# Products with B between the scans of a unit, and a quarter of unit five's product moved to VectorE

## The chip, the cores and the metric

The kernel runs on one core of one Trainium2 chip. The metric is the device time of one execution, in microseconds (us). The core has five engines that run side by side: PE (TensorE, matmuls), DVE (VectorE), ACT (ScalarE), POOL (GpSimd) and SP (SyncE, which here issues the DMAs). Each engine takes its instructions in order; where one engine needs what another makes, it waits on a semaphore.

## The reference

An image batch of shape (8, 64, 64, 96) passes through four layers, each of them added to its input after a group norm. Layers 0 and 2 are two-dimensional selective scans: the image is projected to 192 channels, convolved, and read as a sequence of 4096 positions in four directions; in each direction every channel carries 16 states:

```python
def step(h, inp):
    ut, dt, bt, ct = inp
    dA = jnp.exp(dt[..., None] * A4)
    dBu = (dt * ut)[..., None] * bt[:, :, None, :]
    h = h * dA + dBu
    y = jnp.einsum('bkdn,bkn->bkd', h, ct)
    return (h, y)
```

The four directions are added, normed, gated and projected back to 96 channels. Layer 1 is a scan of the same kind in a chunked form, layer 3 works on upsampled images (matmuls that stand for Fourier transforms). The change touches the scans of layers 0 and 2 alone.

## The kernel before

The images go through the kernel one after another; each has one call of `selective_scan` for layer 0 and one for layer 2, so there are 16 calls. A call has 32 steps: four directions k times eight chunks of 512 positions. A step has six units; a unit is 32 of the 192 channels with their 16 states. The 128 partitions of a unit's tiles are 4 states times 32 channels, and the other factor of 4 states lies along the columns as four groups of 512. A group has one place more, which carries the state in from the chunk before (`SEG` = 513).

A unit t, counted through all steps, with n = t % 6, takes these operations:

- `enter(t)` (ACT) writes the carried states into the free places of the tile `db`, which has three buffers.
- `spread(t)` (PE, L826) repeats the 32 rows of `du` (delta times u) over 128 partitions with a selection matrix, into the PSUM tile `pu`. `pu` has one buffer (pool `p_misc`, tag `misc`).
- `with_b(t)` (L832) multiplies that with B (tile `b`) into `db`, all four groups in one instruction of 128x2048. DVE does this for units 0, 1, 3 and 4, out of `pu`. POOL does it for units 2 and 5 (`n % 3 == 2`); POOL does not read PSUM here but takes `du2`, a copy of the rows 64 to 95 of `du` that goes to DRAM (`dud`) and comes back four times repeated by DMA.
- `decays(t, p)` (ACT, L847) writes the exponentials of two groups into `da[p]`. There is one `da` for each half p.
- `scan(t, p)` (DVE, L862) runs the recurrence over the two groups of half p, with `da[p]` and `db`, into `h`, which has five buffers.
- `leave(t)` keeps the last states (ACT, L878) and multiplies `h` with C (POOL, L883).

`total_y(i, hf)` (PE, L890 and L900) adds the states of units 3 hf to 3 hf + 2 of step i up: first one matmul that brings in what y holds, then 12 matmuls with the matrix `red`, each from 128 partitions to 32. Unit q of the three writes the band of rows 32 q to 32 q + 31 of the PSUM tile `py`. ACT copies `py` to `y` (L1001, L1011). The 12 are issued group by group, the three bands of a group next to each other.

`prepare(i)` is a generator that makes a step's inputs in eight parts: two matmuls into `pv` (L733, L743) and ACT's copies of them into `raw`, the DMAs that spread B, delta and C (`b`, `dx`, `c`, through DRAM), the softplus of delta (ACT, L767), and, in its seventh part, `du` on POOL (L785, where the chunk runs down columns of the image, otherwise L791) with the DMAs of `dud` and `du2`. `raw`, `du` and `du2` lie in the pool `soft`:

```python
tc.tile_pool(name="chunk", bufs=2) as cp,
tc.tile_pool(name="soft", bufs=1) as tp,
```

so that the next step's `du` is written over the one before. Parts of `prepare(i + 1)` and `prepare(i + 2)` are called in fixed places of the loop; the seventh is called by `leave` of unit 3 (`more`), ahead of unit 3's product with C.

`Beside` is a list of operations of layer 3 of the image before (matmuls on PE with an ACT operation behind each), three or four of which are put into each step. The first image has none, so that two of the 16 calls run without them.

The order on every engine is written out by hand (`tc.manual_schedule()`): it is the order of the calls in the loop over t at the end of `selective_scan`. In it, a unit's two scans stand next to each other on DVE, and a product with B follows behind the second.

Of the kernel before, what the change touches and what calls it, by code (L numbers as in the profile page):

```python
# [22 lines left out]
LC = 512  # L23
# [3 lines left out]
NSG = 4  # L27
# [40 lines left out]
def tile_vision_stack(  # L68
# [20 lines left out]
    nc = tc.nc  # L89
# [360 lines left out]
    def near(t, wh, at, n):  # L450

        if not wh:
            return t[:, at : at + n]
        return t.rearrange("p (h w) -> p h w", w=64)[:, :, at // 64 : (at + n) // 64]
# [5 lines left out]
    def cut(t, wh):  # L460

        return t.rearrange("p (w h) -> p w h", h=64) if wh else t
# [217 lines left out]
    def selective_scan(w, wdt, dgw, a, d, u, y, beside):  # L680
# [22 lines left out]
        total = len(steps) * units  # L703
        with (
# [11 lines left out]
            made = {}  # L716
            pool, ops = beside
            pool[0] = bp

            def prepare(i):  # L720

                k, c = steps[i]
                wh, at = k % 2 == 1, c * LC
                uv = [near(u[:, hf, :], wh, at, LC) for hf in range(2)]
                m = made[i] = {"dx": [], "du": []}
# [64 lines left out]
                else:  # L790
                    nc.gpsimd.tensor_mul(du, raw[:DM], u[:, :, at : at + LC])  # L791
                m["du"] = du
                dud = dp.tile([32, 2, LC], F32, name="dud")
                nc.sync.dma_start(dud, du[64:96])
                m["du2"] = du2 = tp.tile([128, 2, LC], F32, name="du2")
# [5 lines left out]
            def groups(t):  # L801

                return t[:, 1:].rearrange("p (g s) -> p g s", s=SEG)[:, :, :LC]
# [17 lines left out]
            def spread(t):  # L821

                m, n = made[t // units], t % units
                rows = slice(32 * (n % 3), 32 * (n % 3) + 32)
                m["pu"] = pu = pmp.tile([128, LC], F32, name="pu", tag="misc")
                nc.tensor.matmul(pu, sel[rows, :], m["du"][rows, n // 3, :], start=True, stop=True)  # L826

            def with_b(t):

                m, n = made[t // units], t % units  # L830
                pool = n % 3 == 2
                (nc.gpsimd if pool else nc.vector).tensor_mul(  # L832
                    groups(m["db", n]),
                    (m["du2"][:, n // 3, :] if pool else m["pu"])
                    .unsqueeze(1)
                    .to_broadcast([128, NSG, LC]),
                    m["b"],
                )

            def decays(t, p):  # L840

                i, n = t // units, t % units
                k, _ = steps[i]
                dst = das[p][:, 1:].rearrange("p (g s) -> p g s", s=SEG)
                for g in range(2):
                    gs = 2 * p + g
                    nc.scalar.activation(  # L847
                        dst[:, g, :LC],
                        made[i]["dx"][n // 3][:, n % 3, :],
                        AF.Exp,  # L850
                        scale=av4[:, k, n, gs : gs + 1],
                    )

            def scan(t, p):
                i, n = t // units, t % units
                k, _ = steps[i]
                rev = int(k >= 2)
                way = slice(None, None, -1) if rev else slice(None)
                at = slice(2 * p * SEG + rev, 2 * (p + 1) * SEG + rev)
                if p == 0:  # L860
                    made[i]["h", n] = gp.tile([128, NSG * SEG + 1], F32, name="h", bufs=5)
                nc.vector.tensor_tensor_scan(  # L862
                    made[i]["h", n][:, at][:, way],
                    das[p][:, rev : 2 * SEG + rev][:, way],
                    made[i]["db", n][:, at][:, way],
                    0.0,
                    ALU.mult,
                    ALU.add,
                )

            def leave(t, more):

                i, n = t // units, t % units
                k, _ = steps[i]
                h = groups(made[i]["h", n])
                if n == 0:
                    states[i] = stp.tile([128, NCG * NSG], F32, name="state")
                nc.scalar.copy(  # L878
                    states[i][:, NSG * n : NSG * n + NSG], h[:, :, 0 if k >= 2 else LC - 1]
                )  # L880
                if more:
                    prepare_part(i + 1)
                nc.gpsimd.tensor_mul(h, h, made[i]["c"])  # L883

            def total_y(i, hf):

                k, c = steps[i]
                wh = k % 2 == 1
                py = pyp.tile([128, LC], F32, name="py", tag="py")[:DM]
                nc.tensor.matmul(  # L890
                    py,
                    skip[:, hf, :] if k == 0 else ident[:DM, :DM],
                    near((u if k == 0 else y)[:, hf, :], wh, c * LC, LC),
                    start=True,
                    stop=False,
                )
                hs = [groups(made[i].pop(("h", 3 * hf + q))) for q in range(3)]
                for g in range(NSG):
                    for q in range(3):
                        nc.tensor.matmul(  # L900
                            turn_back(py[32 * q : 32 * q + 32, :], wh, LC),
                            red,
                            cut(hs[q][:, g, :], wh),
                            start=False,
                            stop=(g == NSG - 1),
                        )
                py = py.rearrange("p (h w) -> p h w", h=64) if wh else py
                return near(y[:, hf, :], wh, c * LC, LC), py

            going = {}  # L910

            def prepare_part(i):
                if i < len(steps):
                    if i not in going:
                        going[i] = prepare(i)
                    next(going[i], None)
# [26 lines left out]
                prepare_part(0)  # L943
            conv_half(5, 1, pmp, "misc")
            conv(w, y, u, (8, 24), 0)
            for _ in range(2):
                prepare_part(0)
            conv_half(6, 0, pyp, "py")
            for t in range(3):
# [16 lines left out]
            for _ in range(3):  # L966
                prepare_part(1)
            conv(w, y, u, (40, 48), 0)
            with_b(0)
            other = Beside(ops)  # L970
            for t in range(total + 2):
                n, i = t % units, t // units
                ahead = t + 1 < total
                quota = (i + 1) * len(ops) // len(steps) - i * len(ops) // len(steps)
                if n == 2 and quota > 1:
                    other.begin(pyp, "py")
                if n in (0, 3) and ahead:
                    spread(t + 1)
                elif n == 1 and t + 2 < total:
                    spread(t + 2)  # L980
                if n == 0 and i > 0:
                    sums = total_y(i - 1, 1)
                elif n == 3:
                    sums = total_y(i, 0)
                elif n == 4:
                    if quota > 3:
                        other.begin(pmp, "misc")
                    if t + 2 < total:
                        spread(t + 2)
                    prepare_part(i + 2)  # L990
                elif n == 5:
                    prepare_part(i + 2)
                if t < total:
                    scan(t, 0)
                    if n % 3 == 0 and t + 2 < total:
                        with_b(t + 2)
                if ahead:
                    decays(t + 1, 0)
                if n == 1:
                    if t > 1:  # L1000
                        nc.scalar.copy(*sums)  # L1001
                    if t < total:
                        other.begin(pyp, "py")
                elif n == 2:
                    other.end()
                    if quota > 2:
                        other.begin(pyp, "py")
                elif n == 3:
                    other.end()
                elif n == 4:  # L1010
                    nc.scalar.copy(*sums)  # L1011
                    other.end()
                if t < total:
                    scan(t, 1)
                    leave(t, n == 3)
                if t + 3 < total:
                    enter(t + 3)
                if ahead:
                    decays(t + 1, 1)
                    if (n + 1) % 3 != 2:  # L1020
                        with_b(t + 1)
                if n in (1, 2):
                    other.end()
                    if n == 2 and quota > 4:
                        other.begin(pyp, "py")
                if n in (4, 5):
                    prepare_part(i + 2)
                if n in (0, 1, 5):
                    prepare_part(i + 1)
            other.flush()  # L1030
            assert other.at == len(ops)
# [813 lines left out]
```

## Time and profile before

| | us |
|---|---|
| median of 3 runs | 26653.47 |
| lowest and highest of them | 26631.27, 26673.9 |
| the profiled execution's own time | 26693.06 |
| its span, first to last instruction | 26691.2 |
| DVE busy | 23982.3 (90%) |
| PE busy | 21984.9 (82%) |
| POOL busy | 21235.6 (80%) |
| ACT busy | 16407.9 (61%) |

The mean granted clock of PE over the span is 0.794 of full speed. In the profile a group's line has the source line, engine, operation, tiles and shapes, the number of instructions, the busy time in us and the mean time of one in ns, and then the time that the engine stood idle ahead of them, with what ended it. A timeline line has the start and the length in us; "x3" says that three instructions in a row were merged. A matmul in 32-bit floats shows as two records of each kind, one for each of two passes: PE for the passes themselves, PEld for the loads of their weights.

### The profile page before, as it was taken

What the parts mean: (1) busy time and instruction counts of PE and PEld (TensorE: products, weight loads), DVE (VectorE), ACT (ScalarE), POOL (GpSimd) and SP (SyncE); (2) the same over time, 40 slices, a digit from 0 to 9 for tenths busy, and PEclk for the clock granted to TensorE, in tenths of its full rate; (3) what the DMA queues carried; (4) which work ended last, traced back from release to release, by engine and by line L of the source; (5) the groups of instructions that cost most, each with busy time, mean ns of one, the idle gap of its engine ahead of it and who ended that gap; (6) DMA issues with size and microseconds to landing.
All of it is one profiled execution on the core that took longest, in us unless ns stands there. A gap on an engine that the chain in (4) does not pass through costs nothing. (4 is left out here: it accounts for less than half of the span.)

```text
span 26691.2 us, 282273 instructions
## 1 busy us (share of the span) xinstructions
PE 21984.9 (82%) x90981; PEld 8484.0 (32%) x90981; DVE 23982.3 (90%) x16689; ACT 16407.9 (61%) x29921; POOL 21235.6 (80%) x7928
## 2 busy tenths in 40 slices
PE   6796788888888878888888887888888888788888
PEld 2151222422224222242223422234222342223424
DVE  9989999898998989889898898988989889898896
ACT  5656566565665656556565565655656556565564
POOL 8949898497975979759797697976979769796694
PEclk7787777877778777787778877788777887778878
DMA  5515454154541545425453254532545325453352
GB/s 125 122 35 129 120 129 109 41 132 123 131 107 47 131 123 132 102 50 133 123 132 97 58 132 123 133 90 62 132 123 132 85 68 133 123 133 78 75 132 68
DMA packets 1678115, 2836.59 MB, mean 106 GB/s; under 512 B 434473, under 2 KB 477769, under 8 KB 1672033
## 3 DMA queue, kind: packets, MB, share of 16 engines
q1 hardware_dynamic: 1660000, 2812.23, 43.3%
q8 instruction: 731, 11.98, 0.2%
q10 hardware_dynamic: 16640, 6.29, 0.1%
q14 instruction: 744, 6.09, 0.1%
HBM read 2390.02 MB, written 427.49 MB: 106 GB/s over the span
## 5 line engine op out<-in xcount | busy, mean ns | idle before, releaser
L862 DVE TENSOR_TENSOR_SCAN h<-da,db 128x1026 f32<-128x1026 f32 x6144 | 13745.7, 2281 | 744.8 <-ACT da L847 378.5
L883 POOL TENSOR_TENSOR h<-h,c 128x2048 f32<-128x2048 f32 x3072 | 12743.1, 4172 | 968.2 <-ACT state L878 528.3
L900 PE MATMUL py<-h,cst 128*32 128x512 f32 x24576 | 5344.6, 749 | 473.0 <-POOL h L883 472.6
L847 ACT ACTIVATE da<-dx,a0s 128x512 f32<-128x512 f32 x6144 | 4239.6, 690 | 1548.8 <-DVE h L862 1373.0
L847 ACT ACTIVATE da<-dx,a2s 128x512 f32<-128x512 f32 x6144 | 4239.2, 690 | 1546.5 <-DVE h L862 1375.0
L832 POOL TENSOR_TENSOR db<-du,b 128x2048 f32<-128x2048 f32 x1024 | 4661.3, 4552 | 306.7 <-DMA du<-dud 226.5
L832 DVE TENSOR_TENSOR db<-pu,b 128x2048 f32<-128x2048 f32 x2048 | 4643.3, 2267 | 141.6 <-PE pu L826 138.2
L826 PE MATMUL pu<-du,cst 32*128 32x512 f32 x4096 | 2940.8, 805 | 1455.7 <-DVE db L832 927.4
L900 PEld LDWEIGHTS py<-h,cst 128*32 128x32 f32 x24576 | 1217.5, 133 | 4997.2 <-issue 3829.7
L826 PEld LDWEIGHTS pu<-du,cst 32*128 32x128 f32 x4096 | 735.2, 223 | 3145.9 <-DVE db L832 1580.8
L743 PE MATMUL pv<-u,wk 96*128 96x512 f32 x2048 | 1290.5, 762 | 388.1 <-ACT raw L738 388.1
L506 PE MATMUL ps<-s,w3as 96*128 96x512 f32 x1344 | 1069.4, 888 | 641.7 <-ACT sf L513 258.9
L1349 ACT ACTIVATE sg<-sg 128x768 f32<-128x768 f32 x1024 | 819.6, 800 | 862.2 <-PE sg L1333 862.2
L890 PE MATMUL py<-y,cst 96*96 96x512 f32 x1536 | 1306.1, 946 | 9.0 <-ACT y L1011 5.7
L733 PE MATMUL pv<-u,wk 96*96 96x512 f32 x2048 | 1200.9, 716 | 59.6 <-DVE u L281 27.4
L1303 POOL TENSOR_TENSOR ce<-ec,cr 112x512 f32<-112x512 f32 x256 | 521.5, 2037 | 754.9 <-ACT ec L1301 736.6
L1381 DVE TENSOR_TENSOR wt<-wt,cbm 128x768 f32<-128x768 f32 x1024 | 990.6, 1001 | 128.9 <-ACT wt L1350 128.1
L878 ACT COPY state<-h 128x4 f32<-128x4 f32 x3072 | 588.6, 192 | 796.5 <-DVE h L862 788.2
L526 PE MATMUL ps<-w3bs,sf 128*128 128x96 f32 x5376 | 1071.5, 356 | 0.0
L314 POOL TENSOR_SCALAR xn<-xs,sb 96x512 f32<-96x512 f32 x192 | 204.8, 1069 | 997.9 <-PE pz L319 440.8
L526 PEld LDWEIGHTS ps<-w3bs,sf 128*128 128x128 f32 x5376 | 992.9, 270 | 0.0
L738 ACT COPY raw<-pv 96x512 f32<-96x512 f32 x512 | 297.6, 581 | 970.1 <-PE pv L733 943.5
(238 smaller groups left out, 29900.9 us busy)
## 6 DMA issues: line engine op xcount, KB each, us to landing
dx<-dd SPq DMA_DIRECT2D x4096, 192.0 KB
b<-bcd SPq DMA_DIRECT2D x2048, 256.0 KB
c<-bcd SPq DMA_DIRECT2D x2048, 256.0 KB
du<-dud SPq DMA_DIRECT2D x2048, 128.0 KB
dd<-raw SPq DMA_DIRECT2D x1024, 192.0 KB
dud<-du SPq DMA_DIRECT2D x512, 128.0 KB
xd<-xs SPq DMA_DIRECT2D x256, 192.0 KB
cr<-bcd SPq DMA_DIRECT2D x1536, 32.0 KB
```

What stands on the lines that cost most here:

```text
L506: nc.tensor.matmul(ps, w3as[:, m * 128 : (m + 1) * 128], live["x2"], start=True, stop=True)
L526: nc.tensor.matmul(po, live["f"][m][:, at : at + 128], w2q[:, m, :], start=False, stop=(m == 2),)
L733: nc.tensor.matmul(pv[:DM], weights[k][:, hi, 128:], uv[hi], start=(hi == 0), stop=(hi == 1))
L743: nc.tensor.matmul(pv, weights[k][:, hi, :128], uv[hi], start=(hi == 0), stop=(hi == 1))
L826: nc.tensor.matmul(pu, sel[rows, :], m["du"][rows, n // 3, :], start=True, stop=True)
L832: (nc.gpsimd if pool else nc.vector).tensor_mul(groups(m["db", n]), (m["du2"][:, n // 3, :] if pool else m["pu"]) .unsqueeze(1) .to_broadc ...
L847: nc.scalar.activation(dst[:, g, :LC], made[i]["dx"][n // 3][:, n % 3, :], AF.Exp, scale=av4[:, k, n, gs : gs + 1],)
L862: nc.vector.tensor_tensor_scan(made[i]["h", n][:, at][:, way], das[p][:, rev : 2 * SEG + rev][:, way], made[i]["db", n][:, at][:, way], 0. ...
L883: nc.gpsimd.tensor_mul(h, h, made[i]["c"])
L890: nc.tensor.matmul(py, skip[:, hf, :] if k == 0 else ident[:DM, :DM], near((u if k == 0 else y)[:, hf, :], wh, c * LC, LC), start=True, st ...
L900: nc.tensor.matmul(turn_back(py[32 * q : 32 * q + 32, :], wh, LC), red, cut(hs[q][:, g, :], wh), start=False, stop=(g == NSG - 1),)
L1381: nc.vector.tensor_mul(it["wt"], it["wt"], m["cbm"][:, j : j + 1, :].to_broadcast([128, RK, Q]),)
```

## The change

Four things are changed.

1. The loop is written anew, so that a product with B stands on DVE between the two scans of each unit. Units 1 and 4 keep one instruction for all four groups; the products of units 0 and 3 are cut into two halves of two groups (`low`, `high`), which stand between the scans of the two units ahead of theirs.
2. Of unit five's product POOL makes three groups (`front`), and DVE makes the fourth (`last`), behind the second scan of unit 3. It reads `pu`, so that PE has one spread more in each step: after unit four's, in iteration n = 3.
3. `total_y` issues its 12 matmuls band by band, and is a generator that stops after two of the three bands; the third is issued later. Unit five's spread stands between them, and unit zero's follows behind the third band.
4. `prepare` has nine parts: `du` is a part of its own, called by `leave` of unit 2 in place of unit 3 and ahead of unit 2's product with C; `dud` and `du2` come at the end of iteration 5. Other parts and the operations of `Beside` have new places in the loop, and `Beside` no longer uses the `misc` tile.

The core of the diff:

```diff
                 m["du"] = du
+                yield
                 dud = dp.tile([32, 2, LC], F32, name="dud")
...
+            low, high, last, front = slice(0, 2), slice(2, 4), slice(3, 4), slice(0, 3)
+
+            def with_b(t, part=slice(None)):
                 m, n = made[t // units], t % units
-                pool = n % 3 == 2
+                pool = n % 3 == 2 and part != last
+                out, b = groups(m["db", n])[:, part], m["b"][:, part]
...
-                hs = [groups(made[i].pop(("h", 3 * hf + q))) for q in range(3)]
-                for g in range(NSG):
-                    for q in range(3):
+                for q in range(3):
+                    h = groups(made[i].pop(("h", 3 * hf + q)))
+                    for g in range(NSG):
                         nc.tensor.matmul(
...
+                    if q == 1:
+                        yield
                 py = py.rearrange("p (h w) -> p h w", h=64) if wh else py
-                return near(y[:, hf, :], wh, c * LC, LC), py
+                yield near(y[:, hf, :], wh, c * LC, LC), py
...
+                if n == 0:
+                    with_b(t + 2)
+                    if i > 0:
+                        adding = total_y(i - 1, 1)
+                        next(adding)
+                elif n == 3:
+                    adding = total_y(i, 0)
+                    next(adding)
+                elif n == 5:
+                    prepare_part(i + 2)
+                scan(t, 0)
...
+                if n == 0:
+                    with_b(t + 1)
+                    prepare_part(i + 1)
                 elif n == 1:
                     other.begin(pyp, "py")
+                    with_b(t + 2, low)
+                elif n == 2:
+                    other.end()
+                    with_b(t + 1, high)
+                    spread(t + 2)
...
                 elif n == 3:
+                    with_b(t + 2, front)
+                    with_b(t + 1)
+                    spread(t + 2)
+                    sums = next(adding)
                 elif n == 4:
...
+                        with_b(t + 2, low)
+                elif n == 5:
+                    prepare_part(i + 2)
+                    if ahead:
+                        with_b(t + 1, high)
                         spread(t + 2)
+                scan(t, 1)
+                if n == 3:
+                    with_b(t + 2, last)
+                    if t + 3 < total:
+                        spread(t + 3)
+                if n == 0:
+                    spread(t + 3)
+                    if i > 0:
+                        sums = next(adding)
...
+                leave(t, n == 2)
+                if ahead:
+                    decays(t + 1, 1)
...
                 elif n == 5:
-                    prepare_part(i + 2)
-                if n in (0, 1, 5):
                     prepare_part(i + 1)
+                    prepare_part(i + 1)
```

## The prediction

> **What bounds the kernel now.** I read the page first, then the scan line's source view, then the timelines of DVE, POOL and PE in one stretch. From the page, engines (busy us, share) and the five groups of the scan loop (group | busy, mean ns | idle before):
>
> ```profile
> PE 21984.9 (82%) x90981; PEld 8484.0 (32%) x90981; DVE 23982.3 (90%) x16689; ACT 16407.9 (61%) x29921; POOL 21235.6 (80%) x7928
> L862 DVE TENSOR_TENSOR_SCAN h<-da,db 128x1026 f32<-128x1026 f32 x6144 | 13745.7, 2281 | 744.8 <-ACT da L847 378.5
> L883 POOL TENSOR_TENSOR h<-h,c 128x2048 f32<-128x2048 f32 x3072 | 12743.1, 4172 | 968.2 <-ACT state L878 528.3
> L900 PE MATMUL py<-h,cst 128*32 128x512 f32 x24576 | 5344.6, 749 | 473.0 <-POOL h L883 472.6
> L832 POOL TENSOR_TENSOR db<-du,b 128x2048 f32<-128x2048 f32 x1024 | 4661.3, 4552 | 306.7 <-DMA du<-dud 226.5
> L832 DVE TENSOR_TENSOR db<-pu,b 128x2048 f32<-128x2048 f32 x2048 | 4643.3, 2267 | 141.6 <-PE pu L826 138.2
> ```
>
> Per step that is 12 scans and 4 products with B on DVE, 6 products with C and 2 with B on POOL. The source view of L862 gives first and last scan of a layer, once without the spectral work beside it, once with it:
>
> ```profile
> L862 DVE TENSOR_TENSOR_SCAN h<-da,db x384: 2266/2270/2296, 117.3 to 1274.2; 128x1026 f32<-128x1026 f32 x192
> L862 DVE TENSOR_TENSOR_SCAN h<-da,db x384: 2266/2271/2297, 3353.1 to 4540.3; 128x1026 f32<-128x1026 f32 x192
> ```
>
> 32 steps take 1159.2 us (36.2 a step) and 1189.5 us (37.2). Two layers are of the first kind; the last of the others (25098.1 to 26299.7) takes 1201.6. Over 16 layers I use 37.2 a step and 512 x 37.2 = 19050 us of the 26691. Now one step, DVE, then POOL:
>
> ```profile
> 1003.12 2.27 DVE L832 TENSOR_TENSOR db<-pu,b 128x2048 f32<-128x2048 f32 x1
> 1005.49 4.48 DVE L862 TENSOR_TENSOR_SCAN h<-da,db 128x1026 f32<-128x1026 f32 x2
> 1009.88 2.27 DVE L832 TENSOR_TENSOR db<-pu,b 128x2048 f32<-128x2048 f32 x1
> ...
> 1041.73 4.48 DVE L862 TENSOR_TENSOR_SCAN h<-da,db 128x1026 f32<-128x1026 f32 x2
> ```
>
> ```profile
> 1009.02 4.54 POOL L832 TENSOR_TENSOR db<-du,b 128x2048 f32<-128x2048 f32 x1
> 1013.53 2.87 POOL L785 TENSOR_TENSOR du<-raw,u 96x1024 f32<-96x1024 f32 x1
> 1016.36 12.42 POOL L883 TENSOR_TENSOR h<-h,c 128x2048 f32<-128x2048 f32 x3
> 1028.75 4.53 POOL L832 TENSOR_TENSOR db<-du,b 128x2048 f32<-128x2048 f32 x1
> ```
>
> Start to start a scan costs 2.20 us, a product on DVE 2.37; 12 x 2.20 + 4 x 2.37 = 35.9, and the step is 36.24: DVE is full. POOL needs 6 x 4.13 + 2 x 4.51 + 2.83 = 36.6 (36.1 where du is the 2.38 us of L791), so both engines bound the step, and POOL may lag a few us because h has five buffers. PE has slack, and its rows show two things that matter later:
>
> ```profile
> 1005.44 2.07 PE L826 MATMUL pu<-du,cst 32*128 32x512 f32 x2 [6.57 <-DVE db L832]
> 1016.45 1.12 PE L826 MATMUL pu<-du,cst 32*128 32x512 f32 x2 [1.51 <-POOL du L785]
> ...
> 1011.10 0.19 PEld L900 LDWEIGHTS py<-h,cst 128*32 128x32 f32 x3 [0.66 <-issue]
> 1011.95 0.19 PEld L900 LDWEIGHTS py<-h,cst 128*32 128x32 f32 x3 [0.66 <-issue]
> 1013.48 0.12 PEld L900 LDWEIGHTS py<-h,cst 128*32 128x32 f32 x3 [0.48 <-issue]
> 1013.91 0.12 PEld L900 LDWEIGHTS py<-h,cst 128*32 128x32 f32 x3 [0.32 <-issue]
> ```
>
> The x3 is one pass of the three row bands of py, run together; a pass takes 0.85 us at first and 0.43 later. The windows view gives a clock of 0.50 for 1003.1 to 1013.2 and 1.00 on both sides. So after 6.6 us of idling PE ran 8 us at half speed.
>
> **The change, part by part.** *Work.* POOL's product for unit five drops from four groups to three: 4.5 x 1/4 = 1.1 us less per step, POOL 35.0 to 35.5. DVE gets one group (128x512) and runs units zero and three as two halves. No row has these sizes; 2267 ns at 2048 columns and 1001 at 768 (L1381) give 0.57 to 0.75 us for the quarter and 1.13 to 1.25 for a half; I take 0.66 and 1.19, the middles. DVE: 12 x 2.20 + 2 x 2.3 + 4 x 1.19 + 0.66 = 36.4, about what it has. A product between two scans also gives ACT's decays (2 x 0.69) more room, which can save up to the 745 us of idle before L862. By work alone this is between nothing and a small gain.
>
> *The wait that is added.* du lies in pool "soft", which has one buffer. Before, the last reader of a step's du was the spread of unit four, issued ahead of the next du on every engine. Now PE spreads unit five too, in iteration 3, while the next du has moved from iteration 3 to iteration 2, ahead of unit two's product with C. In the built program that du on POOL waits for exactly this spread (PE), and the spread waits for DVE's product of unit four in iteration 3, which frees the only pu buffer. Queued behind du on POOL are unit two's product with C and unit five's three groups. PE's last third of total_y waits for the former, and unit zero's spread stands behind it on PE; DVE waits for that spread in its first half product of iteration 4, and everything after it is in order. So the step closes a loop through four engines, and its length is a sum:
>
> - DVE, first half product of iteration 4 to second half product of iteration 2: 8 scans x 2.20, 4 halves x 1.19, one full 2.3: 24.7.
> - X, from there until unit five's spread is done. On DVE: two scans and a full product, 6.7, then a spread (1.1), 7.8. On PE: spread of unit four, skip product, two thirds of total_y, spread of unit five.
> - POOL: du 2.6 (mean of 2.38 and 2.89), product with C 4.13, hand-overs 0.2: 6.9.
> - S, PE's last third of total_y and unit zero's spread, then 0.3 of hand-over.
>
> *The order inside total_y.* It now runs band by band, so the three bands no longer share a pass. The last third is 4 matmuls of two passes: 8 x 0.43 = 3.4 at full clock, with the spread 1.1: 4.6 with the tail of the last pass. But PE has idled 6.9 us by then, as long as the 6.57 of the row above that led to 8 us of half speed. At half speed all of it is 9. I take 8.0: seven us at half do 3.5 of the work, the rest runs at full. For X on PE at full clock: 1.05 + 1.0 + two bands x 3.43 + 1.1 = 10.0 if the bands follow each other, 6.6 if they still overlap. Half clock in its first 7 us makes up to 13.5 of the former. I take 11.0: one after another, plus 1 for the spectral matmul that is issued there in most layers.
>
> T = 24.7 + 11.0 + 6.9 + 8.0 + 0.3 = **50.9 us per step**. Lower end: PE always at full clock and bands overlapping: 24.7 + 7.8 + 6.9 + 4.6 + 0.3 = 44.3. Upper end: X 13.5, S 9.0: 54.4.
>
> Two page rules bear on this. The Trainium skill, "TensorE: Matmul & The Clock Gate" (What's actually happening), says that one busy window of about 3.4 us restores the full clock, where this trace shows 8.0 us; by the rule S would be some 6.3, an estimate, and T 49.2. The same page (Step-by-step) says matmuls stay in program order, while "TensorEngine Tiling (Array Packing)" (Key Properties) says that tiles run independently; the trace settles only neighbours that use different bands. By the first the bands queue, by the second X is 7.8 and T 47.7.
>
> *The rest.* dud and du2 move from iteration 3 to the end of iteration 5, on SP behind the next b. SP then needs 1023.50 to 1026.9 for bcd and b, and two round trips of about 2 us each: some 9 us after bcd, just when POOL wants du2 for unit two. I take nothing, since PE's path covers it, and 1.5 us a step as the upper bound; that raises the upper end to 55.9. The other moves of prepare keep their order; the prologue has one spread more per layer, 16 x 1.1 us, hidden by the convolution.
>
> **The sum.** 512 x (50.9 - 37.2) = 7010 us on a span of 26691, 33700. The profiled execution (26693) stands 40 us over the median, so I forecast 33670 against 26653. Lower end 512 x (44.3 - 37.2) = 3640: 30300. Upper end 512 x (55.9 - 37.2) = 9570: 36200.
>
> **The rivals.** *Faster: the loop has slack.* If the wait of du fell into time in which POOL is behind anyway, only the work counts. Then the step is DVE's 36.4 or, with halves at 1.13 and no gap after a product, 35.7: 512 x 1.5 = 770 us less, 25900; with 36.4 it is 400 less. For it: POOL is never idle in the stretch shown. It decides once unit zero's spread lands before DVE has done the first scan of iteration 4. Unstalled, DVE gets there 5 us after unit four's product; the loop needs 1.1 + 6.9 + 4.6 = 12.6 even at full clock. 4%.
>
> *The bands still overlap*: X is 7.8 to 10, T 47.7 to 49.9, 32000 to 33200. 25%, inside my range.
>
> *PE's clock stays full*, because py now takes PE 48 x 0.43 = 20.6 us per step instead of 6.9: T 44.3 to 47.5, 30300 to 31900. Against it stand 6.9 us of idling in every step. 10%.
>
> *PE itself is the bound*: py 20.6, skip products 2, five spreads 5.3, the products of prepare 3.9 and the spectral work some 4.5 (the windows view has 975.1 us of PE busy in the second layer above and 783.3 in the first, 6.0 a step at a clock of 0.75) are 36.3 at full clock; with 6.9 of idling, 5 to 7 lost to half-speed starts and 5 in hand-overs that is T 53 to 55.9, up to 36200. 20%.
>
> **How the numbers follow.** The wait is in the program and its length is a sum of measured rows, so slower has 0.95: 0.40 for the bands one after another and T near 50.9, the forecast, and 0.25, 0.10 and 0.20 for the three rivals above. A time within 0.2% (53 us, about what a measurement here can tell from no change) would need the stall to equal the savings: 0.01. Faster 0.04. Nine tenths of the slow cases lie between the two ends above.
>
> **What would show it.** In the new profile: POOL idle before du, released by PE's pu, some 5 to 15 us in every step; DVE idle before the half product of db, released by PE's pu, some 10 us a step, and DVE's share near 70%; rows of py with x8 of one band instead of x3 passes, at 0.85 us first after the wait. I am wrong if POOL still runs without gaps, or if DVE waits elsewhere (before the scan of unit two for POOL's db, say). Bands that start within 10 ns of each other would show the overlap.

## The result, and the profile after

| | us |
|---|---|
| kernel before, median of 4 runs | 26663.69 |
| kernel after, median of 4 runs (37071.08 to 37136.91) | 37089.4 |
| ratio, 95% interval | 1.3914, 1.389 to 1.3938 |
| the profiled execution after: own time, span | 37071.08, 37069.2 |

The kernel is slower, as forecast, and by more than the range allowed (36200). The page after, engines and the groups that answer to those of before (group, busy and mean ns, idle before it and what ended that):

```profile
PE 27724.5 (75%) x92005; PEld 9481.4 (26%) x92005; DVE 24277.8 (65%) x18209; ACT 16603.3 (45%) x29921; POOL 20666.5 (56%) x7928
...
L866 DVE TENSOR_TENSOR_SCAN h<-da,db 128x1026 f32<-128x1026 f32 x6144 | 13829.7, 2278 | 2063.8 <-POOL db L836 1995.1
L887 POOL TENSOR_TENSOR h<-h,c 128x2048 f32<-128x2048 f32 x3072 | 12767.0, 4163 | 3152.2 <-ACT state L882 3131.4
L904 PE MATMUL py<-h,cst 128*32 128x512 f32 x24576 | 11376.3, 694 | 3411.7 <-POOL h L887 3411.7
L836 DVE TENSOR_TENSOR db<-pu,b 128x1024 f32<-128x1024 f32 (+2 forms) x3568 | 5152.7, 1444 | 8966.6 <-ACT y L1006 5213.8
L836 POOL TENSOR_TENSOR db<-du,b 128x2048 f32<-128x2048 f32 (+1 forms) x1024 | 4062.6, 3967 | 4441.7 <-DMA du<-dud 2672.9
```

The busy times of DVE and POOL have hardly moved: 1% more and 3% less. PE has 26% more, mostly because the bands of `py` now share few passes (11376 us instead of 5345), yet it stands idle for a quarter of the span. Idle time is what grew: DVE waits 8966.6 us ahead of its products with B where it waited 142 before, and 2064 instead of 745 ahead of its scans. Both together are 21.5 us in each of the 512 steps. The source view of the scan has the first layer, without spectral work:

```profile
L866 DVE TENSOR_TENSOR_SCAN h<-da,db x384: 2265/2282/2295, 117.7 to 1948.0; 128x1026 f32<-128x1026 f32 x192
```

32 steps take 1830.3 us, 57.2 a step, against 36.2. Over all 16 layers it is 57.6 against 37.2. By the same view the layers with spectral work take little more, 1834 to 1860 us, so a step of the first layer can stand for the others. From the view of waits (us in all, times, longest):

```profile
PE py L904 <- POOL h L887: 3411.7, 514, 7.1
...
POOL du L785 <- PE pu L827: 2359.6, 256, 12.2
POOL du L791 <- PE pu L827: 2144.5, 224, 12.2
```

The last two are the forecast wait, 4504 us or 8.8 a step. The first is PE's idling ahead of its last third of total_y, 6.6 us a time (3411.7 / 514). Now one step, from one `du` to the next. POOL, then DVE:

```profile
1363.22 2.34 POOL L791 TENSOR_TENSOR du<-raw,u 96x1024 f32<-96x1024 f32 x1 [7.50 <-PE pu L827]
1365.52 4.15 POOL L887 TENSOR_TENSOR h<-h,c 128x2048 f32<-128x2048 f32 x1
...
1400.76 4.50 POOL L836 TENSOR_TENSOR db<-du,b 128x2048 f32<-128x2048 f32 x1 [8.93 <-DMA du<-dud]
...
1421.13 2.34 POOL L791 TENSOR_TENSOR du<-raw,u 96x1024 f32<-96x1024 f32 x1 [7.61 <-PE pu L827]
```

```profile
1377.40 1.23 DVE L836 TENSOR_TENSOR db<-pu,b 128x1024 f32<-128x1024 f32 x1 [11.26 <-ACT y L1006]
...
1388.85 2.29 DVE L836 TENSOR_TENSOR db<-pu,b 128x2048 f32<-128x2048 f32 x1 [0.33 <-PE pu L827]
...
1398.18 1.23 DVE L836 TENSOR_TENSOR db<-pu,b 128x1024 f32<-128x1024 f32 x1 [2.66 <-PE pu L827]
...
1405.30 2.29 DVE L866 TENSOR_TENSOR_SCAN h<-da,db 128x1026 f32<-128x1026 f32 x1 [3.69 <-POOL db L836]
1407.51 1.20 DVE L836 TENSOR_TENSOR db<-pu,b 128x1024 f32<-128x1024 f32 x1
...
1421.15 0.69 DVE L836 TENSOR_TENSOR db<-pu,b 128x512 f32<-128x512 f32 x1 [3.68 <-PE pu L827]
```

The numbers in brackets are all the waits of DVE in the step: 11.26 + 0.33 + 2.66 + 3.69 + 3.68 = 21.6 us, and 57.9 less 21.6 is 36.3, the work. PE in the same step, from the last third of total_y to the next spread of unit five:

```profile
1369.73 6.53 PE L904 MATMUL py<-h,cst 128*32 128x512 f32 x8 [6.59 <-POOL h L887]
1376.19 1.12 PE L827 MATMUL pu<-du,cst 32*128 32x512 f32 x2
...
1390.69 6.35 PE L904 MATMUL py<-h,cst 128*32 128x512 f32 x16
1396.97 1.12 PE L827 MATMUL pu<-du,cst 32*128 32x512 f32 x2
...
1408.85 2.04 PE L827 MATMUL pu<-du,cst 32*128 32x512 f32 x2 [7.21 <-DVE db L836]
1410.83 2.02 PE L894 MATMUL py<-y,cst 96*96 96x512 f32 x2
1412.78 7.22 PE L904 MATMUL py<-h,cst 128*32 128x512 f32 x16
1419.92 1.12 PE L827 MATMUL pu<-du,cst 32*128 32x512 f32 x2
```

DVE's 11.26 us are labelled "ACT y", the copy of `py`, but the product reads `pu` and not `y`. The copy ran from 1376.30 to 1376.88; the spread of unit zero ended at 1377.31, 0.09 us before DVE went on, and in this step's other waits for `pu` DVE goes on 0.04 to 0.11 us behind the spread too. So the wait is that of `pu`; 5214 of the 8967 us ahead of the products carry the label.

Following the prediction's own chain: `du` and product with C on POOL 1363.22 to 1369.67; last third of total_y and unit zero's spread on PE to 1377.31; DVE from the first half product of iteration 4 at 1377.40 to the end of the second half product of iteration 2 at 1408.71; PE's spread of unit four, skip product, two bands and spread of unit five to 1421.04; the next `du` at 1421.13.

| term | forecast | measured |
|---|---|---|
| DVE, iteration 4 to iteration 2 | 24.7 | 31.3 |
| X, until unit five's spread is done | 11.0 | 12.3 |
| POOL, du and product with C | 6.9 | 6.5 |
| S, last third and unit zero's spread | 8.0 | 7.6 |
| hand-overs | 0.3 | 0.2 |
| step | 50.9 | 57.9 |

The loop is the one foretold, and four of five terms fit within 1.3 us. The first is 6.6 too short, and its rows say by what: the waits 0.33, 2.66 and 3.69 on DVE, 6.7 together. The experiments take the loop and these waits apart.

### The profile page after: what moved, and what is told of

The parts are those of the page before. It is cut to its first block, busy times and chain, and to the rows that moved or that the text cites. A ratio compares the mean times of both kernels' runs of the same rounds, so it can differ in the third digit from the quotient of the medians.

```text
span 37069.2 us, 287589 instructions
## 1 busy us (share of the span) xinstructions
PE 27724.5 (75%) x92005; PEld 9481.4 (26%) x92005; DVE 24277.8 (65%) x18209; ACT 16603.3 (45%) x29921; POOL 20666.5 (56%) x7928
## 5 line engine op out<-in xcount | busy, mean ns | idle before, releaser
L904 PE MATMUL py<-h,cst 128*32 128x512 f32 x24576 | 11376.3, 694 | 3411.7 <-POOL h L887 3411.7
L836 DVE TENSOR_TENSOR db<-pu,b 128x1024 f32<-128x1024 f32 (+2 forms) x3568 | 5152.7, 1444 | 8966.6 <-ACT y L1006 5213.8
L836 POOL TENSOR_TENSOR db<-du,b 128x2048 f32<-128x2048 f32 (+1 forms) x1024 | 4062.6, 3967 | 4441.7 <-DMA du<-dud 2672.9
L827 PE MATMUL pu<-du,cst 32*128 32x512 f32 x5120 | 3526.1, 774 | 2951.1 <-DVE db L836 2951.1
L904 PEld LDWEIGHTS py<-h,cst 128*32 128x32 f32 x24576 | 2498.3, 125 | 12550.0 <-issue 8689.7
L1006 ACT COPY y<-py 96x512 f32<-96x512 f32 x512 | 297.6, 581 | 8272.7 <-PE py L904 8272.7
L791 POOL TENSOR_TENSOR du<-raw,u 96x1024 f32<-96x1024 f32 x256 | 604.4, 2361 | 2600.3 <-PE pu L827 2144.5
L785 POOL TENSOR_TENSOR du<-raw,u 96x1024 f32<-96x1024 f32 x256 | 729.4, 2849 | 2359.6 <-PE pu L827 2359.6
L733 PE MATMUL pv<-u,wk 96*96 96x512 f32 x2048 | 1050.3, 637 | 310.8 <-ACT sf L513 125.3
L506 PE MATMUL ps<-s,w3as 96*128 96x512 f32 x1344 | 916.3, 769 | 268.7 <-ACT y L1004 117.4
L1367 PE MATMUL sg<-rr,lr 32*128 32x384 f32 x4096 | 851.8, 522 | 18.2 <-POOL rr L1314 14.4
```

The source lines that it names most:

```text
L506: nc.tensor.matmul(ps, w3as[:, m * 128 : (m + 1) * 128], live["x2"], start=True, stop=True)
L733: nc.tensor.matmul(pv[:DM], weights[k][:, hi, 128:], uv[hi], start=(hi == 0), stop=(hi == 1))
L836: (nc.gpsimd if pool else nc.vector).tensor_mul(out, (m["du2"][:, n // 3, :] if pool else m["pu"]) .unsqueeze(1) .to_broadcast([128, out.s ...
L904: nc.tensor.matmul(turn_back(py[32 * q : 32 * q + 32, :], wh, LC), red, cut(h[:, g, :], wh), start=False, stop=(g == NSG - 1),)
L1367: nc.tensor.matmul(live[e]["sg"][:, p, :3, :], m["lr"][rows, 0, :], m["rr"][rows, 3 * p : 3 * p + 3, :], start=True, stop=True,)
```

## The experiments

The theory: the loop through `du` carries most of the loss, and the late `du2` and PE's band order add to it with waits of their own. The rival: the wait of `du` is covered, and opening the loop gives little. Times are medians; a ratio is to the kernel before on the same chip, with its 95% interval. The medians of the kernel before beside the experiments lie between 26658 and 26673 us, so that runs from different chips can be set against each other. "A step" is a difference in time over 512 steps.

**Unit five's spread reads du2.** PE then no longer reads `du` last, and `du` on POOL waits for nothing new.

```diff
-                nc.tensor.matmul(pu, sel[rows, :], m["du"][rows, n // 3, :], start=True, stop=True)
+                du = m["du2" if n == 5 else "du"]
+                nc.tensor.matmul(pu, sel[rows, :], du[rows, n // 3, :], start=True, stop=True)
```

> PE spreads unit five out of du2 (which holds the same rows) in place of du, so that the next du on POOL has no reader of this step left to wait for; all else as changed. Theory A (the loop over du is most of the loss): POOL's idle time ahead of du (4500 us in the changed kernel, 8.8 a step) goes to near nothing; what is left is du2, which comes some 18 to 20 us after the second scan of unit four, and the spread of unit zero behind the third band: 42 to 46 us a step, 29100 to 31200 us in all. Theory B (the band order has made PE the bound, the wait only shows there): over 52 us a step, over 34200.

32454.74 us, ratio 1.2165 (1.213 to 1.2201): 4635 us or 9.0 a step less than the kernel after. In the view of waits no `du` waits for `pu` any more. The time stays above what was expected, because the other waits stay; in one step they are 3.53 us ahead of unit three's half product and 3.63 ahead of the scan of unit two.

**du back in its old place.** The same wait, broken at another point: unit five's spread still reads `du`, but the next `du` is made in iteration 3, behind POOL's three groups.

```diff
                 if n == 3:
                     with_b(t + 2, last)
+                    prepare_part(i + 1)
...
-                leave(t, n == 2)
+                leave(t, False)
```

> One edit to the kernel after: the new first part of prepare (du on POOL) is called in iteration 3 again, behind unit five's spread and POOL's three groups, ahead of unit 3's product with C. Unit five's spread still reads du, so du still waits for it, but neither unit two's product with C nor unit five's groups are queued behind that wait any more. Theory: the loop is closed by the place of du on POOL, not by the fifth spread itself. Then the gain is that of reading du2 instead (9 us of 57.6 a step): 31900 to 33200 us, and POOL's wait for pu ahead of du falls below 3 us a step. Rival: the fifth spread costs the time wherever du stands; then POOL's wait stays near 8.8 us a step and the time above 35500 us.

32434.6 us, ratio 1.2163 (1.2145 to 1.2181), 20 us from the run before. POOL's timeline has `du`, in the step I read, without a wait:

```profile
1298.13 2.87 POOL L785 TENSOR_TENSOR du<-raw,u 96x1024 f32<-96x1024 f32 x1
```

Over the whole run `du` still waits 958 us for `pu`, 1.9 a step, but nothing that PE needs is queued behind it. So it is the place of `du` on POOL, ahead of unit two's product with C, that closes the loop; the fifth spread alone does not.

**The first two bands group by group.**

```diff
-                for q in range(3):
-                    h = groups(made[i].pop(("h", 3 * hf + q)))
+                for qs in ((0, 1), (2,)):
+                    hs = {q: groups(made[i].pop(("h", 3 * hf + q))) for q in qs}
                     for g in range(NSG):
+                        for q in qs:
                         ...
-                    if q == 1:
+                    if 1 in qs:
                         yield
```

> The first two bands of total_y are issued group by group again, the third alone behind them; the wait of du stays. Theory A: unit five's spread comes 4 passes earlier (the changed trace has 12 pass times for 16 records), 1.7 to 3.4 us; DVE's wait for unit three's spread (2.7) goes, but turns into a longer wait for du2: some 55.5 us a step, 35500 to 36500. Theory B: 5 us or more less a step, under 34700.

35915.65 us, ratio 1.3463 (1.3424 to 1.3502): 2.3 us a step, within the range of theory A. DVE's waits that are put down to `pu` fall from 3419 to 2194 us, and those of its scans for POOL's `db` rise from 1995 to 2190.

**dud and du2 right behind du**, as before the change, so that SP issues them ahead of the next B.

```diff
                 m["du"] = du
-                yield
                 dud = dp.tile([32, 2, LC], F32, name="dud")
...
                 elif n == 5:
                     prepare_part(i + 1)
-                    prepare_part(i + 1)
```

> dud and du2 are issued right behind du, as before the change, instead of at the end of iteration 5; the wait of du stays. The changed trace has POOL idle 8.9 us for du2 and DVE then 3.7 us for POOL in a step: if this adds to the loop, 54 us a step, 34900 to 35700. If it only stands beside a PE that is late anyway, under 1 us a step less, 36600 to 37100.

35116.18 us, ratio 1.3163 (1.3125 to 1.3201): 3.9 us a step, so the late `du2` adds to the loop. DVE's scan no longer waits for POOL's `db` (1995 us before the edit), and POOL's wait for `du<-dud` falls from 2673 to 227 us, what it was before.

**Unit five on POOL again, whole**, and no fifth spread.

```diff
-                    with_b(t + 2, front)
+                    with_b(t + 2)
                     with_b(t + 1)
-                    spread(t + 2)
...
-                    with_b(t + 2, last)
```

> Unit five's product with B is POOL's alone again (four groups), and PE makes no fifth spread; the order of the loop and of total_y stays as changed. Theory A: the last reader of du is unit four's spread, ahead of the next du, so the loop is gone as in the run with du2: 43 to 47 us a step, 29600 to 31700, a little over that run since POOL has 1.1 us more. Theory B: over 52 us a step, over 34200.

31538.94 us, ratio 1.1822 (1.1788 to 1.1856), 10.8 us a step less than after and 916 us under the run with `du2` for the spread, where it was expected to be a little over that one. The quarter on DVE costs more than it brings even without its loop.

**Edits together.** First `du2` as source and early; then the first two bands group by group as well.

> Unit five's spread out of du2, and dud and du2 issued right behind du. Alone the first gave 48.4 us a step, the second 53.8. If the du wait, the late du2 and the band order are three prices that add up, the run with the first alone still has DVE waits of 3.2 (unit five's quarter), 1.7 (unit zero), 3.8 (unit three) and 2.8 us (POOL's product for unit two); the last goes: 45 to 46 us a step, 30600 to 31300. If the spread of unit three only gets later in its place, 47 or more, over 31700.

30755.41 us, ratio 1.1536 (1.1503 to 1.157), as expected: 12.4 us a step, 9.0 and 3.9 nearly in full.

> The run before with the first two bands of total_y group by group again. If PE's order is what DVE waits for by now, both waits behind two bands (3.2 and 3.8 us) shrink by 4 passes, 1.7 to 3.4 us each: 39 to 42 us a step, 27600 to 29200. If PE isn't the bound, within 1 us of the run before.

29958.99 us, ratio 1.1237 (1.1205 to 1.127): 1.6 a step more, not the 3 to 6 that were expected.

> Unit five on POOL alone (no fifth spread), du2 early, two bands together: what is left of the change is the products between the scans, the halves and the split of total_y. POOL has 1.1 us more than in the run before, DVE 0.6 and PE 1.1 less. If PE is the bound, 38 to 41 us a step (27100 to 28700), below the run before; if POOL were, above it.

28833.21 us, ratio 1.0815 (1.0784 to 1.0847): with unit five on POOL, early `du2` and two bands together. It is below the run before, and 133 us above the range. The three mends give back 7130 of 10426 us, or 8256 where POOL keeps unit five. So the theory holds for the three causes, and something is left. The rest of the runs look for it.

**Unit zero's spread ahead of the third band**, on top of source, early and two bands:

```diff
                     spread(t + 2)
-                    sums = next(adding)
...
                         spread(t + 3)
+                    sums = next(adding)
```

> The run with du2 as source, early du2 and two bands together, and PE's spread of unit zero issued ahead of the third band instead of behind it. DVE's first half product of iteration 4 then no longer stands behind unit two's product with C and 8 passes: 1.7 to 5 us a step less than the run with two bands together, 36.5 to 39 us a step, 26300 to 27700. If the spread waits for the next du instead, no gain.

29025.65 us, ratio 1.0887 (1.0856 to 1.0919): 1.8 us a step, above the expected range. Against the run with two bands together, DVE's waits for `pu` fell from 3031 us (849 of them labelled "ACT y") to 1717, but those of its scans for ACT's `da` rose from 674 to 846.

**The decays ahead of ACT's copy**, where before has them (iterations 1 and 4):

```diff
-                if n == 1 and t > 1:
-                    nc.scalar.copy(*sums)
-                elif n == 4:
-                    nc.scalar.copy(*sums)
                 if ahead:
                     decays(t + 1, 0)
+                if n == 1 and t > 1:
+                    nc.scalar.copy(*sums)
+                elif n == 4:
+                    nc.scalar.copy(*sums)
```

> On top of the three mends and unit zero's spread ahead of the third band (29026 us): ACT's copy of py in iterations 1 and 4 goes back behind the first decays, where the kernel before has it. DVE's wait for da that followed the copy was 846 us in the waits view, 1.65 us a step. Theory: the copy waits for PE's third band and holds the decays up, so this goes: 28000 to 28500 us. Rival: the decays' delay is covered by the wait for unit zero's spread, and that takes its place: 28800 us or more.

28211.58 us, ratio 1.0579 (1.0561 to 1.0596), as expected: 1.6 us a step. The waits for `da` fall from 846 to 304 us, those for `pu` from 1717 to 1440.

**total_y whole, behind the spreads**, on the kernel of the decays run; and the same with unit five on POOL.

```diff
-                for qs in ((0, 1), (2,)):
+                for qs in ((0, 1, 2),):
...
                     with_b(t + 2)
-                    if i > 0:
-                        adding = total_y(i - 1, 1)
-                        next(adding)
-                elif n == 3:
-                    adding = total_y(i, 0)
-                    next(adding)
...
                         spread(t + 3)
-                    sums = next(adding)
+                    sums = total_y(i, 0)
...
                     spread(t + 3)
                     if i > 0:
-                        sums = next(adding)
+                        sums = total_y(i - 1, 1)
```

> The kernel with decays before the copy, and total_y issued whole again, group by group over all three bands, behind the spreads of units five and zero (iteration 3) and of unit three (iteration 0). DVE still has the quarter of unit five, the products still stand between the scans, du and du2 early. Theory: what is left over the kernel before (about 4.6 us a step at 29026) is PE's order, spreads standing behind matmuls that wait for POOL or run at half clock; then 26500 to 27300 us. Rival: it is the fifth spread and the products between the scans themselves, on the one pu buffer; then 27800 us or more, with DVE's waits for pu still 2 us or more a step.

> As the kernel with total_y whole, but POOL makes all of unit five's product and PE makes no fifth spread: the new order on DVE alone, without the quarter. POOL then has 36.6 us a step of work as before. Theory of PE's order: 26500 to 27500 us, POOL the bound. If the quarter on DVE is worth its 1.1 us of POOL's time, this one is up to 500 us slower than the kernel with the quarter; if the fifth spread costs more than it brings, it is faster than that kernel, as the pair without these mends was (28833 against 29959).

29455.4 us, ratio 1.1048 (1.1031 to 1.1064), and 28119.01, ratio 1.0546 (1.053 to 1.0562). The first fits neither side. From its waits:

```profile
DVE h L866 <- PE py L905: 2061.7, 914, 4.8
```

DVE's waits for `pu` are gone (28 us), as theory had it, yet the time is 1244 us above the kernel with the bands apart. PE now reads `h` so late that the five buffers of `h` run out, and DVE waits for one, 4.0 us a step. The two early bands have a use: they free `h`. The second is 1336 us faster than the first: the quarter on DVE with its spread is a loss here too. In the second DVE waits 1139 us for `h`, so part of the difference is this wait.

**Unit five on POOL, decays ahead of the copy**: the kernel of the decays run with the edit of the run with unit five on POOL.

> The kernel with decays before the copy (28212 us), but POOL makes all four groups of unit five's product and PE makes no fifth spread. Theory: in that kernel the time left over the kernel before (3.0 us a step) is DVE's wait for the fifth spread on the one pu buffer (1440 us in the waits view, 2.8 a step). Then 26600 to 27200 us, POOL with 36.6 us of work a step being the next bound. Rival: the wait is only the nearest of several of equal length, products between the scans needing their spreads sooner than PE can make them; then DVE's waits for pu stay over 1 us a step on the other products and the time is 27500 us or more.

27943.74 us, ratio 1.048 (1.0466 to 1.0494). The theory failed, the rival was right: 1074 us of waits for `pu` stay, and the scans wait 744 us for `da` (304 in the decays run, 379 in the kernel before). The source view, by layers, says where. The kernel with the fifth spread, without spectral work; then this one without, then with spectral work:

```profile
L866 DVE TENSOR_TENSOR_SCAN h<-da,db x384: 2264/2280/2296, 120.3 to 1341.1; 128x1026 f32<-128x1026 f32 x192
```

```profile
L865 DVE TENSOR_TENSOR_SCAN h<-da,db x384: 2267/2282/2296, 117.0 to 1274.9; 128x1026 f32<-128x1026 f32 x192
...
L865 DVE TENSOR_TENSOR_SCAN h<-da,db x384: 2267/2283/2297, 3352.3 to 4634.6; 128x1026 f32<-128x1026 f32 x192
```

Without spectral work this kernel takes 1157.9 us for 32 steps, and before took 1156.9: no difference. With it, 1282.3 against 1187.2, 3.0 us a step more. The other layers with spectral work have 82 to 103 us more each, the 14 together 1327 us, so that all of the 1281 that are left lie there. In the layer shown DVE waits 75.7 us for `pu` and 49.0 for `da`, where it waited 10.1 and 19.8 before the change. The fifth spread with the quarter costs 62.9 us in a layer where nothing else is late, 2.0 a step (1220.8 against 1157.9). Over the whole run it is 268 us, 0.5 a step, so with spectral work it costs less.

**One spectral operation moved** from iteration 2, ahead of the bands, to iteration 5.

```diff
                 elif n == 2:
                     ...
-                    if quota > 3:
-                        other.begin(pyp, "py")
...
                 elif n == 5:
                     ...
+                    if quota > 3:
+                        other.begin(pyp, "py")
...
-                if n == 2:
+                if n == 5:
                     other.end()
```

> The kernel with unit five on POOL and decays before the copy (27944 us), with one edit: the fourth spectral operation of a step is begun in iteration 5, behind unit one's spread, and not in iteration 2, ahead of total_y's first bands. In that kernel the layers without spectral work take 1157.9 us, as before the change (1156.9), and those with it 1282.3 instead of 1187.2, 3.0 us a step more. Theory: the fourth operation delays PE's first two bands, and with them unit zero's spread, which DVE awaits up to 4.2 us a step; without it half or more of this goes: 26900 to 27400 us. Rival: it is the half-speed clock under the bands, or ACT's spectral copies ahead of the decays; then the operation only delays another spread and the time stays above 27700 us.

27777.87 us, ratio 1.0422 (1.0401 to 1.0444): the rival's side. 166 us came back; the same wait now stands ahead of unit three's product (5.30 us in the step I read, where unit zero's had 4.20). This layer now takes 1263.0 us. What holds the 2.4 us a step that it still has over the 1187.2 of the kernel before stays open: the spectral matmuls, the half-speed bands and ACT's spectral copies all stand ahead of a spread or of the decays there, and no run separates them.

| kernel | us | us a step under the kernel after |
|---|---|---|
| after | 37089 | 0 |
| unit five's spread reads du2 | 32455 | 9.0 |
| and du2 early | 30755 | 12.4 |
| and two bands group by group | 29959 | 13.9 |
| and unit zero's spread first | 29026 | 15.7 |
| and decays ahead of the copy | 28212 | 17.3 |
| and unit five on POOL | 27944 | 17.9 |
| and one spectral operation moved | 27778 | 18.2 |
| before | 26664 | 20.4 |

No version beats the kernel before. A second buffer for `du`, the plainest mend, was not tried; it takes 4 KB more per partition (2 x 512 floats). Nor was a second buffer for `pu`.

## Why the prediction was right, and where it was wrong

*Right: the mechanism.* POOL's `du` waits for PE's fifth spread, 8.8 us a step (forecast 5 to 15); DVE waits for unit zero's spread, 11.3 (forecast some 10); DVE's share is 65% (near 70). The first passes of `py` after the wait are at 0.85 us. Two independent edits that open the loop give 9.0 and 9.1 us. But one of the prediction's own signs of being wrong came as well: DVE waits ahead of the scan of unit two for POOL's `db`, 1995 us or 3.9 a step, the first of the waits below.

*Wrong: the DVE term, 24.7.* It was a sum of work, eight scans and their products, and contained no wait. Measured without its waits it is 24.6. With them it is 31.3, and each of them answers to a step of the prediction.

- 3.69 us, scan of unit two for POOL's `db`, released by `du2`. The prediction saw that `dud` and `du2` queue behind the next B and wrote "I take nothing, since PE's path covers it, and 1.5 us a step as the upper bound". PE's path could not cover it: unit two's product is needed inside the DVE term, in series with X and S. The estimate of the delay was short too: some 9 us from the issue of `bcd` until POOL has `du2`, where it took 13.3 (1387.45 to 1400.76). SP's timeline has the rows:

```profile
1389.21 1.73 SPq L756 DMA_DIRECT2D b<-bcd  x4
1390.98 0.43 SPq L795 DMA_DIRECT2D dud<-du  x1
1396.38 1.71 SPq L798 DMA_DIRECT2D du<-dud  x4
```

  Before, `du2` was issued 1.96 us behind `dud`; here it is 5.4. Early issue gave 3.9 us a step, more than twice the bound of 1.5.
- 2.66 us, half product for unit three's spread. In iteration 0 that spread stands behind the skip product and two bands, 1388.74 to 1397.04, and I costed total_y's band order in X and S alone, though it is issued twice a step. The group-by-group run gave 2.3 us over both places, so that it and early issue, each alone, took some 6 us a step off.
- 0.33 us, unit one's spread.

*X, 11.0 against 12.3.* Spread and skip product run at half speed, 2.04 and 2.02 us, where I took 1.05 and 1.0 at full; the spectral matmul for which I added 1 us is not there in this layer. The two bands took 7.1 us, near the 6.9 of the sum, and that was luck: four passes at half speed (0.85 us) and four passes that two bands shared cancel. *S and POOL* fit: S took 7.6 us, with a granted clock of 0.61 over 1369.6 to 1377.3. The rule of the Trainium skill that I weighed ("TensorE: Matmul & The Clock Gate", What's actually happening: one busy window of about 3.4 us restores full speed) would have made S some 6.3, an estimate.

*Range.* Its upper end, 55.9, had X at 13.5 and S at 9.0, both above what came, and it missed all the same, as the step is 57.6: of the DVE term only the 1.5 for `du2` was let vary.

*Work.* A quarter takes 0.69 us, a half 1.21, POOL's three groups 3.42, near the 0.66, 1.19 and 3.4 taken. "Between nothing and a small gain" holds for the halves between the scans: nothing, 1157.9 against 1156.9 us a layer once all else is mended. For the quarter it is a loss of 2.0 us a step there, and of 268 to 1336 us in the four pairs of runs with and without it.

*Rivals.* The loop has no slack. PE is not the bound, with 75% busy and idle in each step until POOL or DVE releases it. The clock does not stay full: it is 0.50 over the first 4 us of X (1408.8 to 1412.8) and 0.61 over S. The bands overlap, but by little: the 16 records of the two bands at 1355.0 start at 12 different times, at four of them in pairs 3 to 6 ns apart.

*Not foreseen.* The prediction counted the spectral operations as one matmul in X and, in one rival, as work of PE; it had no term for their new places in the loop. In the mended kernel, their layers hold all that is left.

## What to carry to other kernels

When a new reader is added to a tile with one buffer, go round the loop through all engines, and put into the sum each wait that stands inside its terms: a term taken from busy times is a lower end, not a middle. "Covered by another path" holds only if that path runs beside the wait; if both are in series in one loop, they add. Before moving an instruction forward in the order of an engine, list what is queued behind it; here the same new reader cost 9 us less a step with `du` behind that queue than ahead of it.

## What the runs showed of the hardware that I had not expected

In these runs matmuls of different bands overlap fully only if they are issued next to each other. In the run with unit zero's spread first, at full clock (1.00 over both rows), two bands group by group and then one band alone:

```profile
1284.73 3.63 PE L905 MATMUL py<-h,cst 128*32 128x512 f32 x16
...
1289.84 3.62 PE L905 MATMUL py<-h,cst 128*32 128x512 f32 x8
```

16 records take what 8 take. Issued band by band, in the kernel after, 16 records have 12 pass times: four single ones, four in pairs, four single ones. Read in the order of issue, the second band started when two matmuls (four records) of the first were still to run, and no sooner. So PE's starts leave the order of issue here, against the plain "in order" at the head of this document, but by some two matmuls at most. The records do not name their band, and no run varies the distance.

The releaser that the view names can be a bystander: the largest single entry of DVE's waits, 5214 us for ACT's copy of `py`, was the wait for `pu`, which ended 0.4 us after the copy. The timeline of both engines settled it.
